# First batch's q and k biases by a product in the bank, f16 and f32r halves of steps in either order, and a new order of all steps

## Chip, core and metric

The kernel runs on one core of one Trainium2 chip. Its time is device microseconds of one execution; a kernel is timed in several executions, and their median is given. A profile is taken of one further execution.

## The reference, cut to what matters

One transformer block in float32 on 16 batches of 512 tokens with 256 features: linear attention with 16 heads of 16, then a feed-forward part of 1024 with weights rounded to -1, 0 and 1. Each part has a residual and a layer norm.

```python
def _kernel_exp(x):                       # over the 16 elements of a head
    return jnp.exp(x - jnp.max(x, axis=-1, keepdims=True))
q, k, v = proj(Wq, bq), proj(Wk, bk), proj(Wv, bv)
q_kern, k_kern = _kernel_exp(q), _kernel_exp(k)
kv    = jnp.einsum('bhsd,bhse->bhde', k_kern, v)
denom = jnp.einsum('bhqd,bhd->bhq', q_kern, jnp.sum(k_kern, axis=2)) + 1e-06
y     = jnp.einsum('bhqd,bhde->bhqe', q_kern, kv) / denom[..., None]
x = _layernorm(x + (y @ Wo.T + bo))
h = jax.nn.relu(jnp.einsum('bsd,fd->bsf', x, quantize(W1)) + b1)
x = _layernorm(x + jnp.einsum('bsf,df->bsd', h, quantize(W2)) + b2)
```

Weights and biases of q and k are scaled up (by 8 and by some 24), so that the exponentials are sensitive to small errors of the logits.

## The kernel before, in words

A batch is four blocks (t = 0 to 3) of 128 tokens. Precision is kept by splitting: a number is held as a rounded high part (f32r, or f16) and the remainder, its low part, and a product of two such numbers is made as high x high + high x low + low x high. "f32r" operands show as f32 on TensorE in the profile; a true f32 product takes two recorded passes.

Steps of a batch, by name, and the lines of the profile:

- `ldt`, `xt`, `xtl`: load the transposed x, high part (ScalarE), low part (GpSimd or VectorE).
- `qk{t}` (L766, into a PSUM bank `pqk`): six f32r products; in the first batch (b < FB) `qkF{t}_{c}` (L756) instead, two true f32 products per block.
- `mxa{t}` (L776) adds the biases of q and k, `bqk`, while the block is copied from the bank to SBUF; `mxb{t}` (L782) takes the maxima of the heads from SBUF; `mxs{t}` (L786) subtracts them; `ex{t}` (L797) exponentials on ScalarE.
- `ks`, `ksh`, `ksl`, `pks` (L844): sums of the keys over tokens. `dena`, `denb`, `denc`, `nrm`: denominators and the scaled queries `qs`. `g` (L895, L899): x times the keys; `ge` copies it; `kv` (L926), `kvm`, `kvp`, `kvh`, `kvl`: the small matrices of each head; `m` (L954): times Wo.
- `qt`: turns `qs`; `o` (L1163, L1167): product with m. `or`, `nm`, `nq`, `nv`, `np`, `na`: residual and first layer norm (`nm` to `np` and `ya`, `yq`, ... are the same for the second).
- `xt1`: turns the normalised x into `x1T` (f16 high part, f32r low part). In the middle batches this goes by VectorE and two DMA passes; in batch 0 and 15 TensorE turns it (`xt10`, `xt11`, L1027).
- `f{f}` (L1201, bank `ph`), f = 0 to 7: hidden features, two f16 products with the high part of `x1T`, then two f32r products with the low part. `ha{f}` (L1207) bias and ReLU in the bank; `hc{f}` the f16 high part of h; `hb{f}` (L1220) the low part.
- `z{f}` (L1240, bank `pz`): four f16 products with h's high part, four f32r with its low part, for the four blocks. In batch 15 `zL{f}_{t}`, one per block: one f16, one f32r.
- `zr`, `ym`, `yq`, `yv`, `yp`, `ya`, `st`: residual, second layer norm, store. In batch 15 these are done per block on VectorE (statistics L1085, means L1098, variance L1110, scaling L1131) and GpSimd (power, L1120).

Startup: `lqk`, `wh`, `wl` load Wq and Wk and split them; `warm` multiplies a matrix of ones ten times while the loads are under way; `lbqk` loads the two biases into row 0 of a zeroed `bqk`; `pbqk` (L536) spreads them over all partitions by a true f32 product with ones, and `bqke` copies that back to `bqk`. `lwo`, `woh`, `wol` split Wo; `lw`, `sa`, `sg`, `sr`, `tot`, `half`, `qz`, `qc` load W1 and W2 and round them.

All order is written out by hand: the table `ORDER` gives each step of each batch a place in one list over all batches, `OTHER` says for which batches a step runs on its second engine (VectorE for GpSimd, and so on), and the recorder adds a dependency of each instruction on the one before it on its engine. So every engine, and SP's queue of loads and stores, works in list order. There are eight PSUM banks, two of each kind; `ph` has two, `pqk` and the turns share two.

Of the kernel before, what the change touches and what calls it, by code (L numbers as in the profile page):

```python
# [50 lines left out]
WARM = (9, 1)  # L51
GROUPS = {"s": 2, ("y", 15): 4, ("s", 15): 4}
OTHER = {
    "wol": (0,),
    "mxs0": (0, 1, 4, 8, 9, 11, 12),
    "ks": (0, 5, 9, 10),
    "bvm": (0,),
    "kvl": (0, 1, 2, 3, 5, 6, 7, 8, 9, 10, 11, 12, 14),
    "nrm1": (0, 2, 4, 5, 6, 7, 8),
    "xtl0": (2, 5, 8, 12, 14),  # L60
    "xb0": (0, 1, 2, 7, 8),
    "ksl": (1, 2, 3, 4, 6, 7, 9, 10, 11, 12, 13, 14, 15),
    "nm0": (0, 3, 6, 8, 10, 12, 14),
    "nv0": (0, 1, 5, 9, 11),
    "qc3": (0,),
    "qc0": (0,),
    "mxs1": (2, 4, 7, 13),
    "xb1": (1, 2, 3, 5, 8, 10),
    "mxs3": (2, 6, 9, 10),
    "kvp": (1, 5, 6, 8, 9, 10, 11, 12, 13, 14),  # L70
    "qc1": (0,),
    "ek1": (2, 3, 5, 6, 9, 10, 11, 13, 14, 15),
    "x1b1": (0, 3, 6, 10, 14),
    "qc4": (0,),
    "x1b0": (0, 8, 9, 14),
    "qtbl1": (2, 3, 5, 6, 11, 13),
    "qtbl0": (2, 4, 6, 9, 11, 13, 14, 15),
    "xt1bl1": (1, 4, 9, 11, 12, 13, 14),
    "ek0": (3, 4, 5, 6, 7, 9, 13),
    "ym0": (0, 4, 5, 7, 8, 9),  # L80
    "hc5": (1, 6),
    "ya2": (0, 7, 12, 13),
    "na2": (2, 3, 11, 12, 13, 15),
    "na1": (2, 3, 4, 9),
    "ya0": (0, 4, 7, 9, 12, 13),
    "xsl0": (4, 5, 11, 12, 14),
    "xsl1": (4, 15),
    "hc7": (1, 6, 8, 11, 12, 13, 14, 15),
    "hc6": (1, 5, 9, 12, 15),
    "hc3": (2, 4, 14),  # L90
    "yv0": (2, 3, 4, 8, 9, 10),
    "nrm0": (6, 10, 11, 13, 14),
    "xt1bl0": (4, 5, 10),
    "hc4": (4, 7, 10, 12, 14),
    "xtl1": (9, 11, 12),
    "na3": (5, 6, 7, 10, 13, 15),
    "hc2": (4, 5, 11, 12, 14),
    "hc0": (5, 7, 8, 9, 10),
    "na0": (6, 7, 9, 14, 15),
    "ya3": (4, 8, 9, 10, 11, 13),  # L100
    "hc1": (10, 12, 14),
    "mxs2": (15,),
    "ya1": (12,),
# [6 lines left out]
    "lwo": (4,),  # L110
    "wh1": (5,),
    "wh0": (6,),
    "wl1": (7,),
    "warm0": (8,),
    "warm1": (9,),
    "woh": (10,),
    "wol": (11,),
    "qkF0_0": (12, 0, 0, 0, 0, 0, 0, 0, 0, 0, 0, 0, 0, 0, 0, 0),
    "qkF0_1": (13, 0, 0, 0, 0, 0, 0, 0, 0, 0, 0, 0, 0, 0, 0, 0),
    "wl0": (14,),  # L120
    "lbqk": (15,),
    "ldt0b": (16, 0, 0, 0, 0, 0, 0, 0, 0, 0, 0, 0, 0, 0, 0, 0),
    "pbqk": (17,),
    "bqke": (18,),
    "mxa0": (19, 125, 179, 322, 420, 503, 623, 748, 962, 1162, 1270, 1344, 1465, 1645, 1810, 2041),
    "mxb0": (20, 126, 180, 324, 426, 557, 664, 749, 963, 1163, 1279, 1384, 1504, 1666, 1859, 2042),
    "qkF2_0": (21, 0, 0, 0, 0, 0, 0, 0, 0, 0, 0, 0, 0, 0, 0, 0),
    "ldt1": (0, 22, 79, 87, 212, 235, 522, 558, 746, 733, 1045, 919, 1226, 1348, 1411, 1597),
    "xt1": (0, 23, 80, 148, 260, 401, 523, 616, 811, 866, 1073, 1252, 1250, 1378, 1617, 1739),
    "xtl1": (0, 24, 81, 181, 294, 448, 555, 704, 812, 867, 1087, 1272, 1301, 1436, 1631, 1774),  # L130
    "qkF1_0": (25, 0, 0, 0, 0, 0, 0, 0, 0, 0, 0, 0, 0, 0, 0, 0),
    "mxs0": (26, 129, 202, 325, 476, 599, 665, 777, 964, 1164, 1280, 1387, 1521, 1667, 1884, 2068),
    "qkF1_1": (27, 0, 0, 0, 0, 0, 0, 0, 0, 0, 0, 0, 0, 0, 0, 0),
    "mxa1": (28, 115, 176, 296, 346, 576, 593, 752, 886, 1050, 1179, 1360, 1575, 1704, 1857, 1979),
    "ldt1b": (29, 0, 0, 0, 0, 0, 0, 0, 0, 0, 0, 0, 0, 0, 0, 0),
    "qkF2_1": (30, 0, 0, 0, 0, 0, 0, 0, 0, 0, 0, 0, 0, 0, 0, 0),
    "ldt0": (0, 31, 107, 93, 257, 379, 539, 437, 723, 600, 905, 1173, 1126, 1459, 1304, 1777),
    "mxa2": (32, 56, 151, 233, 406, 507, 620, 821, 998, 1025, 1288, 1329, 1496, 1582, 1721, 1871),
    "xt0": (0, 33, 108, 154, 258, 380, 540, 606, 773, 842, 1034, 1174, 1299, 1530, 1539, 1809),
    "xtl0": (0, 34, 140, 199, 278, 433, 570, 641, 819, 883, 1040, 1175, 1319, 1557, 1580, 1829),  # L140
    "lw0_2": (35,),
    "exF0": (36, 138, 0, 0, 0, 0, 0, 0, 0, 0, 0, 0, 0, 0, 0, 0),
    "sa0_2": (37,),
    "lw0_1": (38,),
    "sa0_1": (39,),
    "sg0_1": (40,),
    "lw0_0": (41,),
    "sa0_0": (42,),
    "lw0_3": (43,),
    "mxb1": (44, 123, 177, 297, 347, 577, 640, 843, 923, 1120, 1244, 1398, 1576, 1705, 1861, 1996),  # L150
    "mxs1": (45, 134, 207, 318, 422, 618, 649, 848, 924, 1135, 1273, 1410, 1577, 1710, 1874, 2002),
    "exF1": (46, 135, 0, 0, 0, 0, 0, 0, 0, 0, 0, 0, 0, 0, 0, 0),
    "sa0_3": (47,),
    "mxb2": (48, 58, 155, 315, 464, 527, 691, 822, 999, 1026, 1289, 1334, 1544, 1591, 1735, 1873),
    "mxs2": (49, 90, 239, 316, 475, 554, 716, 838, 1000, 1062, 1345, 1386, 1566, 1660, 1799, 1891),
    "exF2": (50, 116, 0, 0, 0, 0, 0, 0, 0, 0, 0, 0, 0, 0, 0, 0),
    "qkF3_0": (51, 0, 0, 0, 0, 0, 0, 0, 0, 0, 0, 0, 0, 0, 0, 0),
    "qkF3_1": (52, 0, 0, 0, 0, 0, 0, 0, 0, 0, 0, 0, 0, 0, 0, 0),
    "mxa3": (53, 60, 214, 330, 484, 568, 728, 767, 863, 1063, 1181, 1431, 1460, 1592, 1736, 1992),
    "mxb3": (54, 99, 215, 331, 487, 573, 743, 802, 1008, 1144, 1182, 1432, 1483, 1684, 1788, 1993),  # L160
    "qk2": (0, 55, 149, 227, 398, 491, 617, 755, 961, 1024, 1199, 1318, 1495, 1579, 1720, 1862),
    "sr0": (57,),
    "qk3": (0, 59, 213, 329, 428, 567, 727, 761, 860, 1041, 1176, 1310, 1402, 1584, 1673, 1968),
    "lbo": (61,),
    "tot0": (62,),
    "half0": (63,),
    "mxs3": (64, 100, 217, 332, 488, 586, 744, 834, 1009, 1153, 1266, 1449, 1510, 1685, 1844, 2000),
    "exF3": (65, 137, 0, 0, 0, 0, 0, 0, 0, 0, 0, 0, 0, 0, 0, 0),
    "ks": (66, 139, 243, 352, 512, 657, 763, 877, 1029, 1169, 1347, 1453, 1595, 1728, 1926, 2081),
    "sg0_2": (67,),  # L170
    "qz2": (68,),
    "ldx": (69, 128, 78, 251, 447, 363, 621, 884, 938, 1150, 1227, 1435, 1497, 1643, 1795, 1982),
    "gF0": (70, 169, 0, 0, 0, 0, 0, 0, 0, 0, 0, 0, 0, 0, 0, 0),
    "lbv": (71,),
    "sg0_3": (72,),
    "ksh": (73, 160, 249, 354, 513, 658, 764, 878, 1061, 1184, 1362, 1484, 1596, 1741, 1933, 2093),
    "ksl": (74, 161, 261, 371, 526, 669, 765, 922, 1075, 1190, 1367, 1485, 1603, 1759, 1934, 2099),
    "pks": (75, 162, 265, 372, 533, 696, 766, 956, 1109, 1204, 1373, 1508, 1626, 1778, 1950, 2108),
    "qz1": (76,),
    "lwv": (77,),  # L180
    "lw1_0": (82,),
    "sa1_0": (83,),
    "sg1_0": (84,),
    "gF1": (85, 170, 0, 0, 0, 0, 0, 0, 0, 0, 0, 0, 0, 0, 0, 0),
    "bvm": (86,),
    "ge": (88, 185, 308, 432, 579, 680, 800, 979, 1151, 1271, 1430, 1574, 1668, 1772, 1997, 2143),
    "dena": (89, 171, 267, 388, 543, 697, 788, 958, 1110, 1207, 1403, 1509, 1640, 1780, 1951, 2109),
    "lw1_1": (91,),
    "sa1_1": (92,),
    "lb1": (94,),  # L190
    "sc0": (95,),
    "lw1_3": (96,),
    "sa1_3": (97,),
    "qk0": (0, 98, 178, 270, 353, 449, 601, 745, 891, 1161, 1201, 1343, 1464, 1644, 1794, 2040),
    "denb": (101, 172, 268, 397, 544, 702, 794, 959, 1111, 1208, 1405, 1511, 1641, 1787, 1953, 2110),
    "denc": (102, 174, 274, 404, 548, 705, 798, 965, 1112, 1225, 1406, 1542, 1642, 1804, 1955, 2123),
    "nrm0": (103, 198, 290, 410, 562, 719, 803, 973, 1136, 1240, 1413, 1543, 1659, 1813, 1970, 2125),
    "kvb": (104, 196, 266, 374, 538, 731, 778, 957, 1138, 1206, 1424, 1567, 1683, 1779, 1952, 2173),
    "kv": (105, 186, 323, 441, 594, 711, 815, 994, 1170, 1302, 1468, 1599, 1744, 1796, 1998, 2156),
    "kvm": (106, 188, 327, 444, 595, 732, 816, 995, 1171, 1303, 1475, 1600, 1760, 1798, 1999, 2174),  # L200
    "lw1_2": (109,),
    "kvp": (110, 218, 333, 445, 637, 740, 826, 997, 1172, 1316, 1507, 1625, 1761, 1846, 2001, 2175),
    "kvh": (111, 219, 334, 453, 638, 741, 844, 1006, 1193, 1317, 1545, 1656, 1775, 1847, 2020, 2178),
# [194 lines left out]
def block_kernel(ctx: ExitStack, tc: tile.TileContext, x, xT, wqT, wkT, wvT, woT,  # L398
# [84 lines left out]
    def startup_steps():  # L483
# [40 lines left out]
        for c in range(EC):  # L524
            qk_weight_steps(c)


        @step("lbqk")
        def _():
            for j, bias in enumerate((bq, bk)):  # L530
# [801 lines left out]
```

## Time and profile before

| | |
|---|---|
| median of 3 runs | 477.89 us (477.59 to 477.92) |
| the profiled execution | 477.44 us, of which the span from first to last instruction is 475.6 |
| granted TensorE clock, mean | 0.998 |
| busy: PE, DVE, ACT, POOL | 464.8, 442.6, 409.0, 368.0 us |
| share of the chain that ended last: PE | 65% (pz 19, ph 19, pqk 10, po 7, pg 6) |
| mean of one `mxa`, one `mxb` | 679, 679 ns |

PE is TensorE, PEld its weight loads, DVE VectorE, ACT ScalarE, POOL GpSimd, SP the queue of loads and stores. Matmuls are pipelined: the time of one from record to record is shorter than its own duration, so times of steps are read from start to start.

### The profile page before, as it was taken

The numbers are of one execution on the slowest core, as the hardware profiler recorded it, in microseconds if no ns is written. First come the engines' busy times: TensorE is split into PE (matmuls) and PEld (weight loads), VectorE is DVE, ScalarE is ACT, GpSimd is POOL, SyncE is SP. The second block draws the span as 40 slices with busy tenths as digits, with TensorE's granted clock in tenths as the row PEclk, the third lists the DMA queues.
The fourth block names the chain that finished last, engine by engine and source line by source line (L and its number), as shares of the span: only waits on it lengthen the run. The fifth ranks groups of instructions, "written<-read, shape, count | busy, mean of one in ns | idle before, by whom it ended". The sixth has DMA issues, their size and how long they took to land.

```text
span 475.6 us, 8979 instructions
## 1 busy us (share of the span) xinstructions
PE 464.8 (98%) x2964; PEld 377.2 (79%) x2964; DVE 442.6 (93%) x866; ACT 409.0 (86%) x908; POOL 368.0 (77%) x383
## 2 busy tenths in 40 slices
PE   9999999999999999999999999999999999999995
PEld 6777888788797888878888787888887888878764
DVE  3999999999999999999999999999999999988856
ACT  4988987978979999998988889888998998987773
POOL 3669698879989899788598798899997578854423
PEclk9999999999999999999999999999999999999999
DMA  7902045260523544344362435333454053252012
GB/s 231 364 26 87 3 150 160 90 198 25 183 83 109 159 156 141 125 129 137 113 200 82 142 112 168 121 110 135 133 146 143 38 171 106 87 162 62 1 45 88
DMA packets 35666, 58.52 MB, mean 123 GB/s; under 512 B 4130, under 2 KB 21796, under 8 KB 35620
## 3 DMA queue, kind: packets, MB, share of 16 engines
q1 hardware_dynamic: 35332, 57.69, 38.0%
q8 instruction: 23, 0.38, 0.3%
q10 hardware_dynamic: 288, 0.26, 0.2%
q14 instruction: 23, 0.19, 0.1%
HBM read 34.87 MB, written 23.07 MB: 122 GB/s over the span
## 4 chain that ended last, share of the span: by engine, by line
PE 65%; POOL 4%; DVE 1%; issue 1%; DMA 1%; ACT 0%; POOLq 0%; SPq 0%; DVEq 0%
PE pz L1240 19%; PE ph L1201 19%; PE pqk L766 10%; PE po L1167 7%; PE pg L899 6%; PE pkv L926 2%; PE pm L954 2%; DMA wx1T<-rx1T 1%; DMA dx1T<-wx1T 1%; POOL x L909 1%; POOL xs_6l L738 1%; PE pks L844 0%; POOL qk L786 0%; POOL qT_4l L1019 0%; POOL qs L876 0%
## 5 line engine op out<-in xcount | busy, mean ns | idle before, releaser
L1207 ACT ACTIVATE ph<-ph,b1s,scl 128x512 f32<-128x512 f32 x128 | 95.3, 746 | 20.4 <-PE ph L1201 19.6
L786 POOL TENSOR_TENSOR qk<-qk,mx 128x512 f32<-128x512 f32 x48 | 54.4, 1139 | 7.5 <-DVE mx L782 7.1
L776 DVE TENSOR_TENSOR qk<-pqk,bqk 128x512 f32<-128x512 f32 x64 | 43.2, 679 | 2.8 <-ACT bqk L540 2.0
L797 ACT ACTIVATE ex<-qk 128x512 f32<-128x512 f32 x64 | 40.0, 629 | 5.3 <-POOL qk L786 2.8
L782 DVE TENSOR_REDUCE mx<-qk 128x32 f32<-128x512 f32 x64 | 43.3, 679 | 1.0
L1182 POOL TENSOR_TENSOR x1b<-x,b_bc 128x512 f32<-128x512 f32 x23 | 30.2, 1318 | 5.5 <-DVE h_1l L1220 5.5
L1101 ACT ACTIVATE junk_o<-x,nm_o 128x256 f32<-128x256 f32 x64 | 31.9, 501 | 0.7 <-POOL nm_o L1091 0.3
L1101 ACT ACTIVATE junk_z<-x1b,nm_z 128x256 f32<-128x256 f32 x60 | 30.1, 504 | 2.8 <-POOL nm_z L1091 2.7
L1201 PEld LDWEIGHTS <-w1f 128*128 128x128 f16 x256 | 16.0, 98 | 20.3 <-issue 17.1
L909 POOL TENSOR_TENSOR x<-x,bo_bc 128x512 f32<-128x512 f32 x21 | 28.3, 1349 | 2.8 <-DVE xs_4l L738 2.6
L1075 DVE SCALAR_TENSOR_TENSOR x1b<-pz,scl,x1b 128x256 f32<-128x256 f32 x64 | 28.2, 475 | 1.0 <-PE pz L1240 0.5
L1136 ACT ACTIVATE x1b<-x1b,nmr_z,rstd_z 128x256 f32<-128x256 f32 x43 | 24.1, 596 | 5.7 <-POOL nmr_z L1122 5.7
L876 POOL TENSOR_TENSOR qs<-ex,rden 128x512 f32<-128x512 f32 x20 | 23.6, 1187 | 4.5 <-DVE rden L868 4.4
L1136 ACT ACTIVATE x<-x,nmr_o,rstd_o 128x256 f32<-128x256 f32 x43 | 23.6, 594 | 1.5 <-POOL nmr_o L1122 1.3
L1075 DVE SCALAR_TENSOR_TENSOR x<-po,x 128x256 f32<-128x256 f32 x64 | 24.4, 415 | 0.3 <-PE po L1167 0.2
L1120 POOL TENSOR_TENSOR rstd_z<-var_z,expo 128x4 f32<-128x4 f32 (+1 forms) x19 | 18.7, 988 | 3.9 <-DVE var_z L1110 2.4
L820 POOL TENSOR_TENSOR ks<-ex 128x512 f32<-128x512 f32 x12 | 15.6, 1296 | 7.4 <-ACT ex L797 7.2
L1120 POOL TENSOR_TENSOR rstd_o<-var_o,expo 128x4 f32<-128x4 f32 x16 | 19.9, 1246 | 1.3 <-ACT var_o L1114 0.6
L863 DVE TENSOR_REDUCE den<-dent 128x64 f32<-128x1088 f32 x16 | 20.5, 1282 | 0.3
L848 DVE TENSOR_TENSOR dent<-ex,pks 128x1024 f32<-128x1024 f32 x16 | 19.4, 1211 | 0.6 <-PE pks L844 0.4
L984 DVE STREAM_TRANSPOSE rx1T<-x 128x1024 f32<-128x1024 f32 x14 | 17.4, 1241 | 1.2 <-ACT x L1136 0.7
L984 DVE STREAM_TRANSPOSE rqT<-qs 128x1024 f32<-128x1024 f32 x14 | 17.3, 1239 | 0.5 <-POOL qs L876 0.4
(887 smaller groups left out, 1893.5 us busy)
## 6 DMA issues: line engine op xcount, KB each, us to landing
x<-in_x_dram SPq DMA_DIRECT2D x16, 512.0 KB, 4.3
xt<-in_xT_dram SPq DMA_DIRECT2D x30, 256.0 KB, 4.0
out_dram<-x1b SPq DMA_DIRECT2D x30, 256.0 KB, 2.2
wqT<-rqT SPq DMA_DIRECT2D x14, 512.0 KB, 2.9
wx1T<-rx1T SPq DMA_DIRECT2D x14, 512.0 KB, 2.9
dqT<-wqT SPq DMA_DIRECT2D x56, 128.0 KB, 3.0
dx1T<-wx1T SPq DMA_DIRECT2D x56, 128.0 KB, 3.5
w<-in_w1T_dram SPq DMA_DIRECT2D x4, 256.0 KB, 5.8
```

What stands on the lines that cost most here:

```text
L766: nc.tensor.matmul(s.pqk[t], s.xt[i][:, c, tt], wqk[j][:, c, :], start=(c == 0 and n == 0), stop=(c == EC - 1 and n == 2))
L776: nc.vector.tensor_tensor(s.qk[t].rearrange("p g d -> p (g d)"), s.pqk[t], bqk, ALU.add)
L782: nc.vector.tensor_reduce(s.mx[t], s.qk[t], AX.X, ALU.max)
L786: engine(f"mxs{t}", b, nc.gpsimd, nc.vector).tensor_tensor(s.qk[t], s.qk[t], s.mx[t].unsqueeze(2).to_broadcast([P, 2 * NH, HD]), ALU.subtract)
L797: nc.scalar.activation(s.ex[:, t, :], qk, AF.Exp)
L1075: nc.vector.scalar_tensor_tensor(out=r, in0=p[t], scalar=scl[:, 2:3] if key == "z" else 1.0, in1=r, op0=ALU.mult, op1=ALU.add, **{} if las ...
L1101: nc.scalar.activation(junk, getattr(s, what)[:, t, :], AF.Square, bias=n.nm[:, t:t + 1], accum_out=stat("sq")[:, t:t + 1])
L1120: nc.gpsimd.tensor_tensor(stat("rstd")[:, sl], n.var[:, sl], expo[:, sl], ALU.pow)
L1136: nc.scalar.activation(r, r, AF.Identity, bias=nmr, scale=rstd)
L1201: nc.tensor.matmul(s.ph[f], (w1f, w1)[i][:, c, f * P:(f + 1) * P], s.x1T[i][:, c, :], start=(n == 0), stop=(n == 2 * EC - 1))
L1207: nc.scalar.activation(s.ph[f], s.ph[f], AF.Relu, bias=b1s[:, f:f + 1], scale=scl[:, 1:2])
L1240: nc.tensor.matmul(s.pz[t], hx[:, t * P:(t + 1) * P], (w2f, w2)[i][:, f, :], start=(done[tt] == 1 and t == tt[0] and i == 0), stop=(done[t ...
```

## The change

1. First batch: the biases are loaded into rows 0 and 32 of `bqk`, rounded to f32r (`bqkh`, ScalarE), and row 32 is replaced by the remainder (`bqkl`, VectorE). A product of f32r ones with this matrix, `qkB{t}`, is added to each block's bank as its last product. `mxa` goes; `mxb` takes the maxima from the bank; `mxc{t}` copies the bank to SBUF, on ScalarE for blocks 0 and 3, on VectorE for 1 and 2. `pbqk`, still needed by the other batches, is an f32r product of the same matrix.
2. `FLIP` lists the steps `f` and `z` that do their f32r half first and their f16 half second.
3. Batch 15: `z` of f = 0 to 5 is done for two blocks at a time (`zP{f}_{h}`), only f = 6 and 7 per block.
4. `ORDER` and `OTHER` are new throughout, and the warm-up is 7 + 1 products, not 9 + 1.

```diff
-WARM = (9, 1)
+FLIP = {
+    "f0": (0, 1, 3, 5, 8, 9, 10, 11, 12),
+    "f1": (1, 2, 3, 4, 8, 9, 10, 11, 12, 13, 14, 15),
...
+    "z7": (2, 5, 6, 10, 12, 13),
...
+}
+WARM = (7, 1)
...
+    bqkr = const.tile([P, 2 * E], F32R, tag="bqkr", name="bqkr")
...
         @step("lbqk")
         def _():
-            for j, bias in enumerate((bq, bk)):
-                nc.sync.dma_start(out=bqk[0:1, j * E:(j + 1) * E], in_=bias.unsqueeze(0))
+            for row in (0, 32):
+                for j, bias in enumerate((bq, bk)):
+                    nc.sync.dma_start(
+                        out=bqk[row:row + 1, j * E:(j + 1) * E], in_=bias.unsqueeze(0))
+
+        @step("bqkh")
+        def _():
+            nc.scalar.copy(bqkr, bqk)
+
+        @step("bqkl")
+        def _():
+            engine("bqkl", 0, nc.gpsimd, nc.vector).tensor_tensor(
+                bqkr[32:64], bqk[32:64], as32(bqkr[32:64]), ALU.subtract)
...
-            nc.tensor.matmul(halves["b"], ones, bqk, start=True, stop=True)
+            nc.tensor.matmul(halves["b"], onesr, bqkr, start=True, stop=True)
...
-                                     start=(c == 0), stop=(c == EC - 1))
+                                     start=(c == 0), stop=False)
...
+                @step(f"qkB{t}")
+                def _():
+                    nc.tensor.matmul(s.pqk[t], onesr, bqkr, start=False, stop=True)
...
+            else:
+                @step(f"mxc{t}")
+                def _():
+                    qk = logits().rearrange("p g d -> p (g d)")
+                    if engine(f"mxc{t}", b, nc.scalar, nc.vector) is nc.scalar:
+                        nc.scalar.copy(qk, s.pqk[t])
+                    else:
+                        nc.vector.tensor_copy(qk, s.pqk[t])
...
-                nc.vector.tensor_reduce(s.mx[t], s.qk[t], AX.X, ALU.max)
+                raw = s.qk[t] if b >= FB else s.pqk[t].rearrange("p (g d) -> p g d", d=HD)
+                nc.vector.tensor_reduce(s.mx[t], raw, AX.X, ALU.max)
...
+        def halves_of(name):
+
+            return (1, 0) if b in FLIP.get(name, ()) else (0, 1)
...
-                for i in range(2):
+                n = 0
+                for i in halves_of(f"f{f}"):
...
-                for i, hx in enumerate(s.h[f]):
+                order_ = halves_of(name)
+                for i in order_:
...
-                for t in range(T):
-                    z_step(f, f"zL{f}_{t}", ((("z", "zL")[t // 2], (t,)),))
+                for h in range(T // 2):
+                    pair = tuple((("z", "zL")[h], (2 * h + k,)) for k in range(2))
+                    if f < FC - 2:
+                        z_step(f, f"zP{f}_{h}", pair)
+                    else:
+                        for k in range(2):
+                            z_step(f, f"zL{f}_{2 * h + k}", pair[k:k + 1])
```

The list order at the three places that the prediction walks through, TensorE's steps alone (a number after a dot is the batch):

- Start, before: warm, qkF0, pbqk, qkF2 (first half), qkF1, qkF2, qkF3, qk2.1, qk3.1, tot0, g (half 0), pks, g (half 1), qk0.1, kv, qk1.1, sc1, qt0, m, qt1, tot1, o0, qk2.2, o1, qk1.2. After: warm, qkF1, qkF0, qkF2 (first half), qkB0, qkB1, qkF2, qkB2, pbqk, qkF3, qkB3, qk2.1, qk3.1, g (half 0), tot0, g (half 1), pks, qk1.1, qk0.1, kv, tot1, sc1, qt0, m, qt1, qk1.2, o0, o1.
- From o of batch 15 to its turn, before: f4.14, f2.14, z0.14, z1.14, f6.14, f5.14, z2.14, xt10, xt11. After: f2.14, f4.14, z0.14, z1.14, f5.14, z2.14, f6.14, z3.14, xt10, xt11.
- End, before: the last is zL1_1 to zL7_1, the seven of block 1. After: zL6_3, zL7_3, zP5_0, zL6_1, zL7_1, zL6_0, zL7_0, zL6_2, zL7_2.

On SP's queue, before: x of batch 0 (first half), Wk, Wo, the two biases, x of batch 0 (second half) among loads of batch 1. After: a load of batch 1 and the four bias loads come ahead of that second half, and Wo behind two quarters of W1. On ScalarE, after, the magnitudes of those quarters and the conversion of Wo stand ahead of `bqke` and the first batch's exponentials.

## Prediction

> **What bounds the kernel now.** I read the page first: busy shares, then the chain that ended last.
>
> ```profile
> span 475.6 us, 8979 instructions
> ...
> PE 464.8 (98%) x2964; PEld 377.2 (79%) x2964; DVE 442.6 (93%) x866; ACT 409.0 (86%) x908; POOL 368.0 (77%) x383
> ...
> PE   9999999999999999999999999999999999999995
> ...
> DVE  3999999999999999999999999999999999988856
> ```
>
> TensorE is busy in every slice but the last. As busy marks of pipelined matmuls overlap, I then asked for stages, to see where it is idle (second column: PE busy, its instructions in brackets).
>
> ```profile
> 30.00:60.00 30.00, 29.16 (x148) 23.23 (x147) 28.96 (x57) 27.48 (x64) 23.59 (x23) 1.00 0.14 45
> 60.00:440.00 380.00, 379.56 (x2514) 312.52 (x2513) 366.93 (x703) 338.21 (x752) 316.38 (x321) 1.00 0.40 128
> 440.00:450.00 10.00, 9.12 (x63) 6.93 (x62) 7.82 (x21) 7.80 (x22) 4.90 (x8) 1.00 0.00 1
> ...
> 470.00:475.60 5.60, 0.00 (x0) 0.00 (x0) 2.17 (x9) 0.00 (x0) 1.77 (x3) 0.83 0.43 150
> ```
>
> So there are four stages with limits of their own: a start (to about 46 us, first ph step) where TensorE waits for others, a long middle where only its own work counts, a wait at 444 to 449, and 5.6 us of tail without it. Third, the timeline of TensorE alone, for what one step costs.
>
> ```profile
> 200.83 0.61 PE L1240 MATMUL pz<-w2f,h_6h 128*128 128x256 f16 x4
> 201.19 0.72 PE L1240 MATMUL pz<-w,h_6l 128*128 128x256 f32 x4
> 201.75 0.61 PE L1240 MATMUL pz<-w2f,h_7h 128*128 128x256 f16 x4
> 202.12 0.72 PE L1240 MATMUL pz<-w,h_7l 128*128 128x256 f32 x4
> ```
>
> A z step is four f16 products, then four of the f32 form, and the next begins 0.92 us after it: types alternate twice a step.
>
> **The switch of type, the main term.** I took the start times of single matmuls, medians over all steps of a kind. In a z step the first f16 product lasts 120 ns to the next start, the others 109; the f32 ones 118, the last of them 122 when f16 follows and 117.5 when f32 follows; a whole z step between f16 neighbours is 926 ns, where 4 x 109 + 4 x 118 = 908. One round trip f32, f16, f32 thus costs 18 ns. A ph step takes 913.5 ns; its parts without a switch (217 and 234 each, twice) make 901: 12.5 ns. Now all 280 steps (128 ph, 120 z, 32 of the last batch) start a run of f16 of their own; in the changed instruction order there are 162 such runs. 118 round trips x 15 ns = 1.8 us less, all in TensorE's own stream; bounds 118 x 12 = 1.4 and 118 x 18 = 2.1. A part of this is hidden only where TensorE waits anyway.
>
> **Start.** Removed: an f32 bias product (two passes of 0.429, 0.86 us) and two of ten warm-up products (four passes of 213 ns, 0.85). Added: five products of the rounded form at 0.233 (row of pqk), 1.17 us. The first real product can start at 4.68 instead of 5.53; by the landing times its operands are there at 4.2. But warm-up passes take 213 ns where the same 128x128 form of pkv takes 111 at 23 us, and the first pqk pass, from 5.53, lasts 0.69 instead of 0.43: full speed comes at about 6.0 us. So 1.37 instead of 0.52 us of real work run at half speed, and of 0.85 only 0.43 is won. Sum to the first product of batch 1: -0.43 - 0.86 + 1.17 = -0.1 us. The Trainium skill ("TensorE: Matmul & The Clock Gate", Part 1) says that the clock opens after a busy window of about 3.4 us that runs freely, and speaks against cutting the warm-up: were the opening moved by one window, some 1.7 us would be lost, by my estimate from that page; no run here shows such a shift.
>
> The copies: four adds of 0.68 on VectorE become two ScalarE copies (0.59, by the bias copy), two VectorE copies and one subtraction (0.68 each at most, by the row of h low parts): VectorE gains 0.7 us. The maxima read the bank; no row shows that reduction, but VectorE's add from a bank and its reduction from SBUF both take 679 ns, so I take 0.68, bounds 0.6 and 0.8, four times.
>
> What follows I walked by the rows in the new order. The wait for a bias now stands before the four pqk ends; its four small loads are issued at 3.1 to 4.6, land like the old ones (2.6 us later), then ScalarE 0.6, VectorE's subtraction behind the x low part: ready near 9.1, needed at 9.6. Queued behind it on TensorE is everything; 0.5 us of cover, and each us beyond it costs one. On SP's queue a 256 KB load of batch 1 and two more bias loads go ahead of the first batch's second half, 0.43 to issue each: by the landings of before its two pieces come at 7.3 and 9.9, needed at 8.8 and 10.1, so the second has hardly any cover. The pqk of batch 1 starts at 13.5 (13.6 before). ScalarE's two magnitudes and the conversion of wo now wait for loads (near 12.5) ahead of the exponentials; these still end at 16.3, before their products. pks stands behind both pg halves and ends at 20.1, where TensorE is at 21.3 now: the two waits of 0.5 and 0.2 for ksd and 0.7 for the exponentials go. What is late next is kvd (ScalarE near 26.0, GpSimd 0.73): pm at 26.85, about 26.8 now, with one tot product more behind it. By 40 us I get 0.6 us. I take -0.7; bounds -1.5 and +1.5 (ScalarE's loads 2 us later).
>
> **Wait before the last turn.** In batch 15 x must be normalised before its turn:
>
> ```profile
> 446.00 0.59 PE L1201 MATMUL ph<-x1T_14h,w1f 128*128 128x512 f16 x2 [0.26 <-DVE h_2l L1220]
> ...
> 448.60 1.06 PE L1027 MATMUL px1T<-ident,x 128*128 128x128 f32 x8 [0.61 <-issue]
> ```
>
> Start to start, 0.4 us are lost before the first of these and 0.8 before the second. Between po and px1T stand seven steps now, eight after: one step of 0.91 us more cover. I take -0.8, bounds 0 and -1.2.
>
> **Tail.** The chain's last pieces:
>
> ```profile
> 469.15 0.43 DVE bn L1085
> 469.58 0.31 DVE x1b L1131
> 469.89 0.09 DVE mv L1098
> 469.98 0.05 DVE var_z L1110
> 470.03 0.07 issue
> 470.10 1.12 POOL rstd_z L1120 x2
> ...
> 472.22 0.41 DVE x1b L1131
> ```
>
> Before, the last token block has seven pairs of products (1.7 us) alone at the end, and VectorE clears the others meanwhile: from the last matmul's start (469.39) to the last scaling's end, 472.63, are 3.24 us. After, blocks 1, 0 and 2 end 0.47 us apart. Start to start VectorE takes 0.39 for an add, 0.34 statistics, 0.15 means, 0.10 variance, 0.33 scaling, GpSimd 0.6 for a power; in the new order that gives 4.4 us. +1.1, bounds +0.7 and +1.6. The store behind it is the same.
>
> **Middle.** The order of everything is new, and so are the engines of many small parts. By row means VectorE gets 0.5 us more, ScalarE 3.3, of 33 and 67 idle: no new bound. To see waits I summed TensorE's work between a step and the one that needs its result. Least distances between ph and the next use of its bank are 2.27 us (2.03 before), between ph and its z step 2.50 (2.28): as tight as before. Three pkv stand only 0.90 us behind pg, where 1.81 was the least; the copy between takes 0.58. The middle now has 3.2 us of gaps beyond its sums. I take +0.3, bounds -1.0 and +1.8.
>
> **Sum.** -1.8 - 0.7 - 0.8 + 1.1 + 0.3 = -1.9 us: the profiled execution of 477.44 (span 475.6 and 1.8 around it) would be 475.5; the median of the runs, 477.89, stands 0.45 above that execution, so 476.0.
>
> **Rivals.** *Given back (20%).* The switches go, but TensorE waits at those places anyway, or the start gives nothing because ScalarE stands behind the load of wo: then the first term halves (+0.9) and the start is 0: 477.89 - 0.9 - 0.8 + 1.1 + 0.3 = 477.6. For it: 93% VectorE; against: the chain of the middle is nearly all PE. This is also the case in which the change hardly does what it says.
>
> *Low part first (14%).* In 87 ph and 75 z steps the f32 half now comes first, and it needs the low part, which is made last (0.68 us on VectorE after the high one). It is wanted 0.44 us earlier than in the old order. Where the distance is short, the whole stream waits: eight z steps turned so have a distance under 4.4 us, and the first ph of 13 batches. The chain ph, ScalarE 0.75, copy 0.6 to 0.68, subtraction 0.68 needs at least 2.1 us, with other work queued on VectorE easily 4. If seven of these lose 0.44, that is 476.0 + 3.1 = 479.1; if nine do, 480.0. It decides from a sum of 2.9 us. Against it: the distances are no shorter than before, and now the low half is mostly ready in time (0.3 us waited in all for L1220).
>
> **How the numbers follow.** Forecast 66%, with 474.5 to 476.9 from its own bounds; given back 20%, near 477.6; low part first 14%, 479.1 to 480.0. About 0.2%, 0.96 us, is what a measurement of this kernel tells from no change: faster is below 476.93, slower above 478.85. Faster 0.67, same 0.19, slower 0.14. Range 474.4 to 478.7: it takes in the second case whole and leaves out a tenth on each side.
>
> **What would show it.** In the profile after, the z and ph steps of the chain should run as pairs near 0.91 and 1.80 us, pks should end near 20, the turn of batch 15 lose at most 0.4, the last matmul start about 3 us earlier and the tail be longer by one. I am wrong if TensorE's waits for L1286 (the low part of h) or for x1T sum to over 2 us, if the first pqk products wait for the bias, or if a ph step still takes 913 ns beside a neighbour of its own type.

## The result, and the profile after

The changed kernel takes 478.7 us (median of 22 runs, 476.93 to 482.15) against 477.55 beside it (22 runs). The ratio of the means is 1.0031, interval 1.002 to 1.0043 (ratios below are of means too). By the medians it is slower by 1.15 us, where 1.9 less was forecast.

The runs lie in two groups. 12 of the 22, with a mean clock of 0.996 to 0.998, take 476.93 to 478.89 (their median 477.9); the other 10, with 0.990 to 0.994, take 479.56 to 482.15 (480.3). The kernel before has one group. So there are two questions: why the better group is no faster than before, and what makes the other.

The profiled execution of the changed kernel took 476.93 us, the best of all; its page:

```profile
span 475.2 us, 8979 instructions
...
PE 462.5 (97%) x2963; PEld 377.1 (79%) x2963; DVE 443.4 (93%) x869; ACT 410.3 (86%) x919; POOL 367.5 (77%) x371
...
PE   9979999999999999999999999999999999999994
...
DVE  4899999999999999999999999999999999998976
```

TensorE works 2.3 us less (464.8 before), and the span is only 0.4 shorter: the work went, and idle time came. The third slice (24 to 36 us) shows a first piece, a 7. By stages (second column PE busy, its instructions in brackets):

```profile
30.00:60.00 30.00, 29.58 (x148) 23.18 (x147) 29.50 (x60) 26.05 (x61) 26.57 (x24) 1.00 0.19 57
60.00:440.00 380.00, 378.32 (x2515) 312.81 (x2515) 365.14 (x702) 342.30 (x767) 312.37 (x307) 1.00 0.41 127
440.00:450.00 10.00, 10.00 (x73) 7.95 (x72) 9.05 (x24) 7.46 (x21) 4.76 (x9) 1.00 0.14 53
470.00:475.20 5.20, 0.00 (x0) 0.00 (x0) 1.80 (x8) 0.00 (x0) 1.50 (x3) 0.76 0.30 101
```

Before, the middle had 379.56 of 380 busy and 440 to 450 had 9.12. Now the stage at 440 is full, as forecast, and the middle lacks 1.7 us. Who is waited for, from the waits of TensorE in the changed kernel (us in total, times, longest):

```profile
PE pqT L1088 <- DVE half L692: 1.4, 1, 1.4
PE tot L687 <- DVE half L682: 1.1, 2, 0.7
...
PE ph L1266 <- DVE h_4l L1286: 0.6, 1, 0.6
PE ph L1266 <- DVE h_1l L1286: 0.6, 1, 0.6
PE ph L1266 <- DVE h_6l L1286: 0.3, 1, 0.3
```

Two places, then: the first turn of `qs` near 26 us, and three `ph` steps near 346, 405 and 407 us, which had no wait before. The first, in the timeline of TensorE:

```profile
23.57 1.05 PE L987 MATMUL pkv<-g,wv 128*128 128x128 f32 x8
25.36 0.35 PE L687 MATMUL tot<-half,ones 128*128 128x1 f32 x2 [0.74 <-DVE half L682]
25.69 0.35 PE L615 MATMUL psc<-scl,ones 128*128 128x1 f32 x2
27.45 0.63 PE L1088 MATMUL pqT<-ident,qs 128*128 128x128 f32 x4 [1.41 <-DVE half L692]
```

and of VectorE in the same time:

```profile
25.95 0.75 DVE L701 SCALAR_TENSOR_TENSOR w<-mag,half,w 128x512 fp32r<-128x512 f32 x1
26.62 0.68 DVE L828 TENSOR_TENSOR qk<-pqk,bqk 128x512 f32<-128x512 f32 x1
27.22 0.15 DVE L692 TENSOR_SCALAR half<-tot 128x1 f32<-128x1 f32 x1
```

The wait is labelled `half`, the last thing VectorE finished; `half` is no operand of the turn. What it needs is a bank: turns and `pqk` share two, both full of batch 1's blocks, and the first add that empties one (26.62, done at 27.3) stands on VectorE behind the rounding of w (25.95). (With an idle stretch put into the kernel before, below, the same wait is labelled with that add, `qk`.) Before, TensorE waited there 0.96 us.

The tail's chain after:

```profile
465.97 0.52 PE pz L1307 x4
...
467.68 0.37 DVE x1b L1136
...
468.50 0.66 DVE bn L1146 x2
...
469.70 1.17 POOL rstd_z L1181 x2
...
471.86 0.41 DVE x1b L1192
```

Between the last product and the last scaling VectorE now has adds, statistics and scalings of several blocks; from the last matmul's start to the end it is 7.21 us, 6.25 before.

To compare kernels I counted, for each, what TensorE needs from start to start beyond the same price list (the durations of the prediction, 18 ns a round trip). This is called the excess below; in us:

| stage | before | changed | changed, FLIP empty | before, halves by type | changed, filled and middle mended |
|---|---|---|---|---|---|
| 0 to 20 | 1.85 | 1.66 | 2.06 | 1.71 | 2.40 |
| 20 to 40 | 2.28 | 3.70 | 3.66 | 2.28 | 1.54 |
| 40 to 60 | 1.37 | 0.84 | 0.83 | 1.39 | 1.66 |
| 60 to 310 | 2.28 | 1.05 | 1.05 | 3.40 | 1.38 |
| 310 to 440 | 0.63 | 3.24 | 1.69 | 0.80 | 1.40 |
| 440 to the last | 1.40 | 0.57 | 0.16 | 1.80 | 0.57 |
| sum | 9.81 | 11.06 | 9.45 | 11.35 | 8.96 |

The last three columns are experiments; the ten filling products of the last one are counted as work.

### The profile page after: what moved, and what is told of

It reads as the page before. It is cut to its first block, busy times and chain, and to the rows that moved or that the text cites. A ratio compares the mean times of both kernels' runs of the same rounds, so it can differ in the third digit from the quotient of the medians.

```text
span 475.2 us, 8979 instructions
## 1 busy us (share of the span) xinstructions
PE 462.5 (97%) x2963; PEld 377.1 (79%) x2963; DVE 443.4 (93%) x869; ACT 410.3 (86%) x919; POOL 367.5 (77%) x371
## 5 line engine op out<-in xcount | busy, mean ns | idle before, releaser
L847 POOL TENSOR_TENSOR qk<-qk,mx 128x512 f32<-128x512 f32 x50 | 56.0, 1124 | 2.9 <-DVE mx L843 2.7
L1266 PEld LDWEIGHTS <-w1f 128*128 128x128 f16 x256 | 18.1, 98 | 29.6 <-issue 24.4
L828 DVE TENSOR_TENSOR qk<-pqk,bqk 128x512 f32<-128x512 f32 x60 | 40.5, 676 | 0.8 <-PE pqk L815 0.6
L843 DVE TENSOR_REDUCE mx<-qk 128x32 f32<-128x512 f32 x60 | 40.4, 676 | 0.7
L970 POOL TENSOR_TENSOR x<-x,bo_bc 128x512 f32<-128x512 f32 x26 | 35.4, 1362 | 1.6 <-PE pg L956 1.6
L1243 POOL TENSOR_TENSOR x1b<-x,b_bc 128x512 f32<-128x512 f32 x24 | 31.9, 1334 | 1.9 <-DVE x L1199 1.2
L1197 ACT ACTIVATE x<-x,nmr_o,rstd_o 128x256 f32<-128x256 f32 x48 | 26.3, 595 | 5.2 <-POOL nmr_o L1183 5.2
L881 POOL TENSOR_TENSOR ks<-ex 128x512 f32<-128x512 f32 x12 | 17.2, 1430 | 4.6 <-ACT ex L858 4.6
L1181 POOL TENSOR_TENSOR rstd_o<-var_o,expo 128x4 f32<-128x4 f32 x16 | 16.9, 1059 | 4.0 <-ACT var_o L1175 3.2
L987 PEld LDWEIGHTS pkv<-g,wv 128*128 128x128 f32 x128 | 16.2, 191 | 2.2 <-ACT g L979 1.0
```

The source lines that it names most:

```text
L828: nc.vector.tensor_tensor(logits().rearrange("p g d -> p (g d)"), s.pqk[t], bqk, ALU.add)
L843: nc.vector.tensor_reduce(s.mx[t], raw, AX.X, ALU.max)
L847: engine(f"mxs{t}", b, nc.gpsimd, nc.vector).tensor_tensor(s.qk[t], s.qk[t], s.mx[t].unsqueeze(2).to_broadcast([P, 2 * NH, HD]), ALU.subtract)
L970: engine(f"xb{h}", b, nc.gpsimd, nc.vector).tensor_tensor(r, r, bo_bc.unsqueeze(1).to_broadcast([P, 2, E]), ALU.add)
L1181: nc.gpsimd.tensor_tensor(stat("rstd")[:, sl], n.var[:, sl], expo[:, sl], ALU.pow)
L1197: nc.scalar.activation(r, r, AF.Identity, bias=nmr, scale=rstd)
```

## The experiments

Times are medians, each beside runs of the kernel before on the same chip (477.55 to 477.62).

### The groups: again, filled, warmed

Theory A: the idle stretch at 24.5 to 27.4 us lets the clock fall back in about half of the runs. The changed kernel unchanged:

> The changed kernel again, to see its runs beside each other. Its earlier runs went from 476.9 to 482.2 us, with mean granted clocks from 0.998 to 0.990; those of the kernel before stayed within 476.9 to 478.2. Theory A (the clock is taken back to half speed for a window, somewhere after it was granted): two groups, near 477.7 us at a clock of 0.997 to 0.998, and near 480.2 at 0.993 to 0.994, about half of the runs each. Theory B (the runs differ by transfers, and the clock only follows): times spread without steps, and no tie to the clock.

478.52 us (12 runs; ratio 1.0025, interval 1.0011 to 1.0038): eight runs of 477.66 to 478.65 at 0.997 or more, four of 479.65 to 480.71 at 0.992 to 0.995.

```diff
+        def fill_step(k, times):
+            @step(f"fill{k}")
+            def _():
+                if "fill" not in halves:
+                    halves["fill"] = bank("z", [P, S], "pfill")
+                for _ in range(times):
+                    nc.tensor.matmul(halves["fill"][:, 0:P], ones, ones, start=True, stop=True)
+        fill_step(0, 3)     # place 114.5, behind kv
+        fill_step(1, 7)     # place 126.5, ahead of the first turn
```

> TensorE is nearly idle from 24.5 to 27.4 us in the changed kernel (kv, then two tiny products, then a wait for a bank). Here ten products of ones with ones (0.22 us each) are put there, three ahead of tot1 and seven ahead of the first turn. Theory A (the idle stretch makes the clock gate close in those runs whose window falls on it): no runs at 0.993 any more, all near 477.5 to 478.0 at 0.997 or more. Rival A2 (the gate opens late because two warm-up products fewer stand ahead): the two groups stay, 477.7 and 480.2.

478.48 us (11 runs; 1.0019, interval 1.0011 to 1.0028), 477.78 to 479.23, clocks 0.995 to 0.998: the group near 480 is gone, as A says, but the median hardly moved. Its profile is also 1.5 us longer than the changed kernel's best; why the filled runs stand some 0.6 above the better group is taken up under "The middle waits".

```diff
-WARM = (7, 1)
+WARM = (9, 1)
```

> The changed kernel with ten warm-up products again instead of eight. Rival A2 (late opening by the shorter warm-up): one group at 0.997 or more, near 478.0. Theory A (the idle stretch at 25 us): still two groups, each some 0.3 us later than without.

479.44 us (12 runs; 1.0027, interval 1.0014 to 1.004): five near 477.9, one at 478.94, six near 480.0. The length of the warm-up is not the cause. But this profile caught an execution of the upper group (the granted clock is the third number from the end):

```profile
24.84:28.25 3.41, 1.14 (x9) 0.88 (x8) 3.33 (x9) 3.41 (x9) 2.22 (x3) 1.00 0.25 100
28.25:31.66 3.41, 3.41 (x16) 3.31 (x16) 3.15 (x5) 2.58 (x6) 3.41 (x3) 0.50 0.27 85
31.66:35.07 3.41, 3.41 (x17) 2.92 (x17) 1.98 (x7) 3.39 (x7) 0.92 (x1) 1.00 0.75 186
```

TensorE is busy 1.14 of 3.41 us, and then, fully busy, runs 3.41 us at half speed: 1.7 us lost. The clock had opened at 4.36 us, and the half-speed stretch begins 23.89 us later, seven times 3.413.

### The converse: an idle stretch in the kernel before

```diff
-                engine(f"nrm{h}", b, nc.gpsimd, nc.vector).tensor_tensor(
+                for _ in range(4 if (h, b) == (1, 0) else 1):
+                    engine(f"nrm{h}", b, nc.gpsimd, nc.vector).tensor_tensor(
```

> The kernel before, with VectorE repeating one multiplication (qs of the first batch's upper half, the same values again, 0.68 us each) three times ahead of the add that frees the pqk bank near 25.6 us. Theory A: the idle stretch of TensorE before the first qT turn grows from 1.2 to about 3 us, all runs lose about 2.0 us (479.5), and about half of them lose 1.7 to 2.1 us more at a mean clock near 0.993, so that two groups appear at 479.5 and 481.4 in a kernel that had none. Rival (the clock has nothing to do with idle time there): one group at 479.5, clock 0.997.

482.41 us (4 runs; 1.0102, interval 1.0089 to 1.0115), all at 0.990 to 0.994: one group, the upper one. The four multiplications took 4.26 us together, not 2.7, so the stretch was 4.5 us long and no run escaped:

```profile
26.82:30.23 3.41, 0.07 (x1) 0.10 (x2) 3.31 (x5) 0.73 (x2) 1.31 (x1) 1.00 0.00 0
30.23:33.64 3.41, 3.41 (x17) 3.19 (x17) 3.19 (x10) 1.97 (x5) 1.06 (x1) 0.50 0.02 7
```

Again 3.41 us at half speed, beginning 23.89 us after the opening (6.34). An idle stretch alone, here of 4.5 us, makes the lower clock.

### Shortening the stretch by order

```diff
-    "nrm1": (102, ...   "qz2": (118,)     "xt1": (0, 25, 81, 120, ...
+    "nrm1": (123.5, ... "qz2": (128.5,)   "xt1": (0, 25, 81, 121.5, ...
```

> The changed kernel with three steps moved in the hand-written order of the first batch, so that VectorE frees the pqk bank earlier: nrm1 goes behind mxa0 of batch 1, qz2 behind mxa1 of batch 1, and xt1 of batch 3 behind kvh. Theory A (TensorE waits near 26 us for the bank that this add frees; the idle stretch then costs one more window of half clock in about half of the runs): the first qT turn starts near 26.1 instead of 27.45, TensorE's idle time in 20 to 40 us falls from 3.7 to about 2.4, no half-speed window follows, all runs lie in one group with a mean clock of 0.997 or more, and the median is about 476.7 (477.9 of the changed kernel's better runs, less 1.2). Rival (the groups have nothing to do with this stretch): two groups remain, about 2 us apart, each about 1.2 lower, median 477.3. Rival (something else is late next, the low part of kvd): no gain, 478.5.

478.96 us (7 runs; 1.0029, interval 1.0018 to 1.004). The first turn starts at 26.78, but the excess at 20 to 40 us is 4.71. `nrm1` now ends at 27.2, ScalarE's next exponential starts only then (27.32; it writes the buffer that `nrm1` reads), VectorE's second add follows it (27.99), and `qk` of batch 2 starts at 29.52, not 28.98. Its profile has no half-speed window; one of the seven runs has a clock of 0.994. The last rival holds. With `nrm1` left in its place:

```diff
-    "qz2": (118,)     "xt1": (0, 25, 81, 120, ...
+    "qz2": (128.5,)   "xt1": (0, 25, 81, 121.5, ...
```

> The changed kernel with two steps moved: the rounding qz2 on VectorE (0.75 us) goes behind the add mxa1 of batch 1 that it stood ahead of, and on ScalarE the high part of x of batch 3 goes behind kvd's high part. nrm1 stays where it is. Theory A (TensorE's idle stretch at 24.5 to 27.4 us is the wait for the pqk bank, and its length brings the half-speed window): the first qT turn starts at 26.7 instead of 27.45, idle time there falls from 2.6 to 1.9 us, the group of runs near 480 is gone, median 477.0. Rival (1.9 us idle is still too long for the clock): two groups, 477.0 and 479.2. Rival (another wait takes its place, as when nrm1 was moved too): 478.5 or more.

479.31 us (9 runs; 1.0032, interval 1.0022 to 1.0041): two at 478.0 and 478.3 with 0.997, the others at 478.9 to 479.7. The turn waits 0.72 us instead of 1.41, `tot` ahead of it 0.74 as before, and the second rival holds: that is still enough for the clock to fall back. Its two better runs are no better than the changed kernel's: ScalarE, whose order I changed too, waits 0.40 us for `kvm`, and the second add comes at 27.90 again.

### The halves by type, alone and left out

The kernel before with its own order, and a FLIP that orders halves by the neighbours' types (168 runs of f16 instead of 280):

> The kernel before, its order and all else untouched, with the halves of ph and pz steps turned where that joins equal types: 168 f16 runs instead of 280, so 112 round trips fewer. Theory C (each costs 17 to 22 ns of TensorE's own time): 1.9 to 2.5 us faster, near 475.3. Rival (the low part is late where it is wanted first): half of that or nothing, 476.5 to 478, with waits of ph and pz steps for VectorE's low parts of 1 us or more in all.

476.7 us (11 runs; 0.9981, interval 0.9973 to 0.999): faster than both kernels, but 0.85 us, not 2.2. The excess grew by 1.5 us, most of it at 60 to 310 and behind 440; what happened at 60 to 310 is taken up under "The middle waits".

```diff
-FLIP = { "f0": (0, 1, 3, 5, ...
+FLIP = {}
```

> The changed kernel with an empty FLIP: every f and z step does its f16 half first, as in the kernel before, while all else is the changed kernel's. 268 runs of f16 instead of 162. Theory (each round trip of types costs TensorE 20 ns, and nothing else hangs on it): 106 x 20 = 2.1 us slower, about 480.6. Rival, given back (TensorE waits for VectorE at those places anyway): at most 1.0 slower. Rival, low part first (the turned steps wait for low parts): no slower or even faster, since the low part is wanted 0.44 us later.

479.37 us (12 runs; 1.0033, interval 1.0019 to 1.0048); its four runs at 0.997 or more take 477.13 to 478.38, as the changed kernel's better group does, and its profiled span is 475.4 against 475.2. So in the changed kernel 106 round trips, 2.1 us of TensorE's work, bring 0.2. (The medians of all runs are 0.7 apart, as eight of these 12 runs have the lower clock, two of them, at 481, only 0.988; why 0.988 is open.) The list of waits changes too:

```profile
PE pqT L1062 <- DVE half L666: 1.4, 1, 1.4
...
PE ph L1240 <- DVE h_1l L1260: 0.6, 1, 0.6
```

The waits for h_4l and h_6l are gone from the list (the one for h_1l stays, with the f16 half first). Excess at 310 to 440 falls from 3.24 to 1.69, and the sum by 1.6. In both orders, then, most of the time saved came back as idle time of TensorE. That TensorE waited there anyway is not shown: the kernel before has one `ph` wait on its list, of 0.3 us. What came between is taken up under "The middle waits".

### The middle waits

One attempt moved work that was not the cause (an x + bias add behind the low part of h 6), on top of the mended start:

```diff
-    "xb1": (..., 2065, 2180)     "ek0": (..., 1745, ...)   "zr0": (..., 1746, ...)   "zr3": (..., 1747, ...)
+    "xb1": (..., 2074.5, 2180)   "ek0": (..., 1755.2, ...) "zr0": (..., 1755.3, ...) "zr3": (..., 1755.4, ...)
```

> The same as the run with the mended start, and besides two waits of the middle mended: VectorE's subtraction exk of batch 13 and two of the residual adds (zr0, zr3 of batch 9) go behind the low part of h 1 of batch 10, and one x + bias add of batch 14 goes behind the low part of h 6 of batch 12. Theory (the 0.59 and 0.61 us that ph steps wait for a bank at 345.7 and 405.3 are pure loss): 1.2 to 1.5 us less than the run with the mended start, about 475.4, and TensorE's idle time beyond its sums in 310 to 350 and 400 to 440 us falls from 1.45 and 1.4 to about 0.7 each. Rival (given back: VectorE is so full that what is moved is late next): at most 0.4 us less.

479.51 us (5 runs; 1.0042, interval 1.003 to 1.0054). At 310 to 350 the excess falls from 1.45 to 0.72, but at 400 to 440 it rises from 1.37 to 2.50, with a new wait of 0.5 for h_0l: that half was given back. (The subtraction `exk_15l` takes 1.65 us there, and 0.68 in the changed kernel.) What VectorE does there in the changed kernel, in its timeline:

```profile
400.46 1.55 DVE L1008 TENSOR_TENSOR kvd_14l<-kvm,kvd_14h 128x256 fp32r<-128x256 f32 x1
...
403.84 0.68 DVE L1282 CAST h_4h<-ph 128x512 f16<-128x512 f32 x1
404.56 0.69 DVE L1286 TENSOR_TENSOR h_4l<-ph,h_4h 128x512 fp32r<-128x512 f32 x1
```

GpSimd's:

```profile
400.43 1.29 POOL L1080 TENSOR_TENSOR qT_14l<-dqT,qT_14h 128x512 fp32r<-128x512 f32 x1 [4.55 <-ACT qT_14h L1075]
```

and TensorE's:

```profile
405.30 0.59 PE L1266 MATMUL ph<-x1T_12h,w1f 128*128 128x512 f16 x2 [0.61 <-DVE h_4l L1286]
```

The subtraction takes 1.55 us, and 0.41 in six of the seven other batches that have it on VectorE: it starts 0.03 us after one of GpSimd's and ends 0.29 after it. The subtraction `exk_13l` at 342.41 does the same (1.78 us, 0.68 in batches 10, 12, 14 and 15; GpSimd adds from 342.36 for 1.29), ahead of h_1l. The Trainium skill ("SBUF — State Buffer", Who interferes with whom) says that a VectorE instruction with two SBUF inputs and a GpSimd instruction that reads SBUF exclude each other, the later one waiting for the whole of the other; both cases here agree to some 0.1 us (behind GpSimd's end they take another 0.29 and 0.54, alone 0.41 and 0.68), while the subtractions from a bank are not slowed: all 128 of h take 0.63 to 0.69, h_6l too, which begins at 405.88 beside a GpSimd subtraction. So the last experiment, on the filled kernel, takes away the collision of `kvd_14l` and moves `exk_13l` behind h_1l, where its length (1.17) holds up no bank that is wanted:

```diff
     "kvl": (0, 2, 3, 5, 8, 12, 13, 15            # OTHER: on GpSimd
+            , 14),
-    "kvl": (..., 2051, 2179)     "ek0": (..., 1745, ...)   "zr0": (..., 1746, ...)   "zr3": (..., 1747, ...)
+    "kvl": (..., 2049.5, 2179)   "ek0": (..., 1755.2, ...) "zr0": (..., 1755.3, ...) "zr3": (..., 1755.4, ...)
```

> The changed kernel with the ten small products in the idle stretch near 25 us (478.48, no group near 480), and the two waits of the middle mended at their source: kvd's low part of batch 14, which takes 1.55 us on VectorE beside GpSimd's work and 0.41 elsewhere, goes to GpSimd, where there is room; exk of batch 13 (1.78 us beside GpSimd, 0.71 elsewhere) and two residual adds go behind the low part of h 1 of batch 10. Theory (the time that ordering by type saved came back as waits of ph steps for VectorE at 345 and 405 us): TensorE's excess in 310 to 350 and in 400 to 440 us falls from 1.43 and 1.39 to about 0.7 and 0.4, and the median by 1.2 to 1.7 us, to about 477.0. Rival (whatever is moved is late next, as in the run where an x + bias add was moved instead): 478.0 or more.

476.41 us (12 runs, 475.64 to 478.03; 0.9976, interval 0.9965 to 0.9988): 2.1 less than the filled kernel, and the fastest of all kernels run here, though its interval overlaps that of the halves alone. Its waits of over 0.2 us, the warm-up's 1.1 left out, hold no `ph` step any more:

```profile
PE tot L700 <- DVE half L695: 0.4, 1, 0.4
PE pks L918 <- DVE x L1149: 0.4, 1, 0.4
PE pqk L828 <- DVE x1T_0l L1124: 0.3, 1, 0.3
```

and GpSimd does the subtraction in 0.73 us ahead of its own:

```profile
401.35 0.73 POOL L1021 TENSOR_TENSOR kvd_14l<-kvm,kvd_14h 128x256 fp32r<-128x256 f32 x1 [4.02 <-ACT kvd_14h L1017]
```

The excess at 310 to 350 fell from 1.43 to 0.74 and at 400 to 440 from 1.39 to 0.09, 2.0 in all: what the two places cost, they gave back.

Which of the two engines waits differs between runs in which their recorded starts lie 0.01 to 0.08 us apart, too close for the records to say who came first. With FLIP empty, `kvd_14l` meets the same GpSimd subtraction, but GpSimd is the one that waits:

```profile
401.89 0.41 DVE L982 TENSOR_TENSOR kvd_14l<-kvm,kvd_14h 128x256 fp32r<-128x256 f32 x1
401.88 1.57 POOL L1054 TENSOR_TENSOR qT_14l<-dqT,qT_14h 128x512 fp32r<-128x512 f32 x1 [4.71 <-ACT qT_14h L1049]
```

TensorE, which is 1.5 us behind the changed kernel at 403, is only 0.2 behind it at 408. So of the 2.1 us that FLIP saves in the changed kernel, 1.3 go at this one place: VectorE waits with it, GpSimd without it. In the order of before it is `exk_10l`, first in the kernel before, then with the halves by type:

```profile
256.84 0.68 DVE L805 TENSOR_TENSOR exk_10l<-ex,exk_10h 128x512 fp32r<-128x512 f32 x1
256.92 1.74 POOL L1182 TENSOR_TENSOR x1b<-x,b_bc 128x512 f32<-128x512 f32 x1
```

```profile
256.61 1.80 DVE L838 TENSOR_TENSOR exk_10l<-ex,exk_10h 128x512 fp32r<-128x512 f32 x1
256.59 1.27 POOL L1215 TENSOR_TENSOR x1b<-x,b_bc 128x512 f32<-128x512 f32 x1
```

There TensorE is 0.4 us ahead of the kernel before at 258 and 0.4 behind it at 270, so 0.8 of the 1.5 us of added excess lies at this place. These are readings of single profiles; only `kvd_14l` was taken to another engine to try it.

The 0.6 us by which the filled runs stand above the better group is of the same kind. A rounding of w on VectorE meets a GpSimd subtraction near 35 us, in the changed kernel and in the filled one:

```profile
34.82 0.74 DVE L701 SCALAR_TENSOR_TENSOR w<-mag,half,w 128x512 fp32r<-128x512 f32 x1
34.86 1.86 POOL L782 TENSOR_TENSOR xs_2l<-x,xs_2h 128x512 fp32r<-128x512 f32 x1 [0.22 <-ACT xs_2h L776]
```

```profile
35.15 1.88 DVE L714 SCALAR_TENSOR_TENSOR w<-mag,half,w 128x512 fp32r<-128x512 f32 x1
35.18 1.29 POOL L795 TENSOR_TENSOR xs_2l<-x,xs_2h 128x512 fp32r<-128x512 f32 x1 [0.21 <-ACT xs_2h L789]
```

In the five profiles of the changed order where it takes 1.82 to 1.88 us (filled, filled and mended, ten warm-up products, two steps moved, the first attempt at the middle), TensorE falls 0.8 us further behind the changed kernel's profile between 35 and 47; in the other three, where it takes 0.75, it does not. Here nothing was moved to try it.

### The turn of batch 15, and the biases, each alone

```diff
-    "z3": (..., 2280, 0)
+    "z3": (..., 2275.5, 0)
```

> The kernel before with its own order, the f16 and f32r halves ordered by type, and one step z3 of batch 14 moved ahead of the turn of x of batch 15, which is the part of the change that gave the wait before the last turn more cover. Theory (that wait is worth 0.8 us by itself): 0.8 less than with the halves alone, 475.9. Rival (given back: what follows the turn waits for it anyway): 476.5 to 476.9.

476.85 us (11 runs; 0.9983, interval 0.9974 to 0.9991), against 476.7 without the step: nothing. The wait of the turn on its operand (0.5) is gone from the list, but the excess behind 440 fell by only 0.18; in the order of before the step does not buy what it buys in the new one.

Part 1 of the change in the order of before (`bqkh` at 15.2, `bqkl` 15.4, `qkB` 21.5, 27.5, 30.5, 52.5, the copies behind them, `pbqk` at 54.2):

> The kernel before, its order, its ten warm-up products and its halves, with part 1 of the change alone: the first batch's biases loaded into rows 0 and 32, rounded and split, added in the bank by a product each, maxima read from the bank, copies by ScalarE for blocks 0 and 3 and by VectorE for 1 and 2; the product that spreads the biases stands behind the first batch. TensorE: five products of 0.233 for one of 0.86, +0.3 us. Theory (the start is bound by TensorE and by what comes after, so VectorE's 0.7 us less buys nothing): 477.9, within 0.4 of the kernel before. Rival (the prediction's term for the start: waits for ksd and the exponentials of 1.4 us go): 476.6. Rival (the copies and maxima wait for the bias behind TensorE): slower by 0.6 or more, 478.2.

480.43 us (5 runs, clock 0.998 and more; 1.0059, interval 1.0047 to 1.0071), 2.9 slower. The first bias product waits 0.58 us for the subtraction, and the second block of batch 1 waits for ScalarE's copy of the biases out of `pbqk`, which frees that bank and which stood, by my placing, behind the first batch's exponentials:

```profile
18.20 0.50 PE L798 MATMUL pqk<-wqkh,xt_1h 128*128 128x512 f32 x1 [1.69 <-ACT bqk L567]
```

1.7 of the 2.9 is that wait, so this run does not price the part by itself. It shows that the last rival can happen.

## Why the prediction was wrong, step by step

**Switches of type: right in size, wrong in worth.** In the changed kernel a z pair without a switch takes 1.832 us where two single steps took 1.852, and a ph pair 1.805 where two took 1.827: 20 and 22 ns a round trip, above my bound of 18. PE busy fell by 2.3. The steps run as pairs:

```profile
449.14 0.72 PE L1307 MATMUL pz<-w,h_4l 128*128 128x256 f32 x4
449.70 0.61 PE L1307 MATMUL pz<-w2f,h_4h 128*128 128x256 f16 x4
450.15 0.60 PE L1307 MATMUL pz<-w2f,h_5h 128*128 128x256 f16 x4
450.50 0.72 PE L1307 MATMUL pz<-w,h_5l 128*128 128x256 f32 x4
```

But the run with FLIP empty shows 0.2 us of it at the end, and the kernel before with halves by type 0.85. The step that failed is the sentence "all in TensorE's own stream": it follows from few waits in the profile of before, but a stream that gets faster moves VectorE's and GpSimd's work against each other, and 1.3 us in one order and 0.8 in the other came back where a VectorE subtraction now took 1.55 or 1.80 us beside GpSimd instead of 0.41 or 0.68. The rival "given back" had the direction, at half the price, but took the waits to be there already.

**Middle: +0.3 forecast, +1.4 measured** (excess at 60 to 440: 4.29 against 2.91; within the bound of 1.8). The waits are not, as the rival "low part first" had it, for the low part as an operand: those `ph` steps wait for a bank, which the low part's reading sets free. I summed TensorE's distances, but priced VectorE's parts at their means; the two that mattered took 1.55 and 1.78 beside GpSimd. The profile of before has such lengthened parts too (`exk_15l` takes 1.81 at 406.91), and the new order decides which of them stand ahead of a bank. The listed waits for L1286 sum to 1.5 us, under the 2 that the prediction named as a sign of being wrong; the last matmul starts 1.4 us earlier, not 3.

**Start: -0.7 forecast, about +0.2 in the profiled execution, and 2.4 more in ten of 22 runs.** This step failed too. TensorE's own work changed as summed (+1.17 - 0.86 - 0.85), but the excess to 60 us rose from 5.50 to 6.20. `pks` ended at 21, not 20, and `pm` began at 27.83, not at about 26.8. I looked for what is late next among the operands of `pm` and missed the bank of the turn before it. The wait, with the one ahead of it, then cost the half-speed window. I had weighed the page's rule only for the opening of the clock, where the warm-up's length made no difference; it bears on idle time later on.

**Wait before the last turn: right.** Excess behind 440 fell from 1.40 to 0.57, the turn waits 0.2; forecast -0.8. That the step of cover is the reason is not shown: put into the order of before it gained nothing.

**Tail: right.** +0.96 for +1.1.

**Sum.** In the two profiled executions: -2.1 (switches) + 0.2 (start) + 1.4 (middle) - 0.8 (turn) + 1.0 (tail) = -0.3 (118 round trips at the 18 ns that the table counts with), and they differ by -0.5. But the changed kernel's was its best of 22. The better group's median, 477.9, is 0.3 above the kernel before. The other profile from that group (477.66, the changed kernel unchanged) is 0.6 us later from 11 us on and hardly more behind that; its clock opened at 6.30 us instead of 5.07, and that this is the reason was not tried. The median of 478.7 lies above 477.9 because almost half of the runs pay for the clock.

## What to carry to other kernels

Work taken from the busiest engine is worth only what the other engines let through: before counting it, look for the instructions of the second busiest that last longer than their mean, for the engine that started just ahead of them, and for the bank or buffer that they set free. A small shift can change which of two engines waits, so one profile does not price such a saving. Of a wait named after something that is no operand, ask which buffer the instruction writes. And near the start of a kernel, an idle stretch of TensorE of about 2 us can cost as much again after it, in some executions only: a spread of times in two groups with two clocks is the sign.

## What the hardware showed

In the four profiles with a half-speed window, it lasted 3.413 us and began 23.893 us (seven such lengths) after the clock had opened. The opening varied from 4.1 to 6.7 us between executions, so the same idle stretch falls on windows of that grid in different ways; which would explain why only some runs pay; that is read from 14 profiles and not tried by itself. Counted start to start, TensorE did nothing in 0.57, 0.64, 0.90 and 0.98 of the window before the half-speed one; in the changed kernel's profiled execution the emptiest window had 0.55, and no half speed followed. One window of 0.57, near 17 us in the run with the biases alone, was not followed either. With each of the four tiny products of `tot` and `psc` counted as the 0.10 us to the next start, the lowest that was followed (two steps moved) has 0.48 and the changed kernel's 0.50. So this count gives no limit: nearly empty windows were followed by half speed, and among those about half empty it does not tell which are. The Trainium skill ("TensorE: Matmul & The Clock Gate", What's actually happening) describes such a free-running window of 3.413 us, which agrees. In HAM oscillation it gives the rule of no idle gap above about 3.4 us; here less was too much: waits of 0.8 and 1.5 us close together, in the run with ten warm-up products.

The upper group stands 2.1 to 2.4 us above the lower, and one window at half speed loses 1.7. In all three profiles of the changed order with such a window the rounding of w near 35 us took 1.82 to 1.88 us and TensorE lost 0.8 more by 47, which would make up the rest; it was not tried by itself.
